# Ordering the first stage of a graph-network kernel: a second list planner, trace durations and a table of ranks

## The chip, the cores and the metric

The kernel runs on one core of a Trainium2 chip. A core has engines that run side by side, each through its own list of instructions in order: TensorE (PE) for matrix products, VectorE (DVE), ScalarE (ACT) and GpSimd (POOL) for elementwise work, and SyncE (SP), which here only issues DMA transfers. The metric is the device time of one execution in microseconds (us), as the median of several runs.

## The reference

The input is 128 batches of 128 tokens with 128 features (x) and a 0/1 adjacency matrix per batch. Four graph layers follow one another, each applied to a normalized, rectified copy of x and added to x. The first stage of the kernel, which the change is about, computes layer 0 and the first, costly part of layer 1:

```
# layer 0 (only relation 1 can occur in the given data)
h = relu(layernorm(x));  mask = (adj == r)
agg = sum over r of (mask / degree) @ h @ rel_weights[r]
x = x + relu(layernorm(agg + h @ self_w.T + self_b))
# layer 1, first part
h = relu(layernorm(x))
D = abs(h[:, :, None, :] - h[:, None, :, :])     # all pairs of tokens of a batch
p = D @ W1.T + b1                                # 128 features -> 64
m, v = mean and variance of p over all batches and pairs
```

The statistics m and v need all pairs of all batches. So the values of p are stored, and a second stage can start only when the last of them has been counted. The second stage computes the scores, the softmax and the output of layer 1, a third one layers 2 and 3.

## The kernel before

**Groups and tiles.** A group is G = 4 batches, and there are NG = 32 groups. A batch has NT = 4 tiles of pair differences, each [128 features, 2 x 8 x 128 pairs], so a group has 16 tiles, and tile i belongs to batch i // 4 with t = i % 4. As the pairs are symmetric, only about half of them are formed.

**Steps of a tile** (`pairs`, five per tile): "d", the difference of tokens (`difference`, L361; t = 1 and 3 on GpSimd, t = 0 and 2 on DVE, where one operand is read from the PSUM tile XP); "abs", the absolute value on ScalarE (`absolute`, L409), except for t = 0, which takes a maximum in place of the difference; "hp", the products on PE into a PSUM tile (`products`, L371, and for t = 0 also L374, which adds a linear part with weights "xw"); "hs", the copy of that PSUM tile to an SBUF buffer z by ScalarE (`evacuate`, L385); "st", the statistics of z on DVE (`statistics`, L399 to L406). There are two buffers of d for each of the two engines and two PSUM tiles "hp". Each half batch of z is stored to HBM ("out0", "out", L392) out of a ring of ten buffers.

**Steps of a group's chain** (`chain`, and `features` for each half of the group): layer 0 and the normalizing of its result. In order: load x and adj; the mask, moments and roots (GpSimd L493, DVE L483 and L485, GpSimd L272 to L331), the centred copy "hn" (ACT L506), transposes and products on PE with copies by ACT between them ("pt", "hT", "pm", "maskT", "ph", "hw", "po"; L516 to L530), "o", "mvo", "rso", "oc", "on", "end", then "mvx", "rsx" and two steps "h1" (ACT L547). For each half: "xp" (PE, two transposes into XP, L439), "xe" (ACT, copy, L443), "again" (GpSimd, L456), "pw" (PE, L447, into other columns of the same XP bank) and "xw" (ACT, L451, reads these columns). The chain of a later group is worked beside the tiles of an earlier one.

**What sets the order.** Each step is recorded with `step(name, engine, cost, after, rank, work)`. `_ordered` then makes a plan: it keeps a time for each engine, takes the engine that can start earliest, on it the step that can start first, and among those that could start at the same time the one of the lowest rank. A step can start when the steps it names in `after` are done, plus HOP1 = 0.4 us if they ran on another engine. `takes` and `gives` count the two PSUM banks "sm". The plan is the order in which the program issues the instructions, and so the order on each engine. Nothing at run time follows its times. Ranks count tiles: for example, d of tile i has rank i - 2 or i - 3, abs i - 1, hp i, hs i + 1, st i + 2. A step of the chain has s0 plus a number, with s0 = 16 g - 31.

A second planner, `_ranked`, stands in the same file and orders the third stage. It differs in this: an engine becomes free LATE[engine] before a step's end (DVE 0.08, ACT and PE 0.1, GpSimd 0.02 us); the hop is HOPS = 0.1 us; a tile's products count as done DEEP = 0.25 us after their end; a DMA counts as landed after a time by its kind; banks are given as a list of holds (which step takes one, which steps have to read it before it is free); and among the steps that could start within a margin of the first, the lowest rank is taken.

Of the kernel before, what the change touches and what calls it, by code (L numbers as in the profile page):

```python
# [18 lines left out]
G = 4  # L19
# [20 lines left out]
HOP1 = 0.4  # L40
HOPS, DEEP, ARRIVING, NEAR = 0.1, 0.25, 2.4, 0.025
LATE = {"SP": 0.0, "Pool": 0.02, "ACT": 0.1, "DVE": 0.08, "PE": 0.1}
LANDED = {"load": 6.0, "out": 5.0, "out0": 5.0}
# [51 lines left out]


def _ordered(steps, limits, hop):

    named = {s[0]: s for s in steps}
    free, done = dict.fromkeys(("SP", "Pool", "ACT", "DVE", "PE"), 0.0), {}
    left = {tag: [0.0] * n for tag, n in limits.items()}
    waits = {s[0]: [a for a in s[3] if a in named] for s in steps}
    followers, ready = {}, {e: {} for e in free}
    for name, after in waits.items():
        for a in after:
            followers.setdefault(a, []).append(name)
    missing = {name: len(after) for name, after in waits.items()}

    def released(name):
        engine = named[name][1]
        ready[engine][name] = max([0.0] + [done[a] + hop * (named[a][1] != engine) for a in waits[name]])

    for name, n in missing.items():
        if n == 0:
            released(name)
    plan = []
    while len(plan) < len(steps):
        best = None  # L120
        for engine, names in ready.items():
            could = []
            for name, since in names.items():
                takes = named[name][4]
                if all(left[tag] for tag in takes):
                    could.append((max([free[engine], since] + [min(left[tag]) for tag in takes]),
                                  named[name][6], name))
            if could:
                first = min(could)[0]
                one = min((c for c in could if c[0] == first), key=lambda c: c[1])  # L130
                if best is None or first < best[0]:
                    best = one
        start, _, name = best
        _, engine, cost, _, takes, gives, _, work = named[name]
        del ready[engine][name]
        free[engine] = start + cost
        done[name] = start + cost + (LANDING if engine == "SP" else 0)
        for tag in takes:
            left[tag].remove(min(left[tag]))
        for tag in gives:  # L140
            left[tag].append(start + cost + hop)
        plan.append(work)
        for f in followers.get(name, ()):
            missing[f] -= 1
            if missing[f] == 0:
                released(f)
    return plan
# [63 lines left out]
def tile_gnn_stack(ctx: ExitStack, tc: tile.TileContext, a: dict, out: bass.AP):  # L211
# [96 lines left out]
    def two_stages(general):  # L308
# [6 lines left out]
        with tc.tile_pool(name="c0", bufs=1) as c0, tc.tile_pool(name="p0", bufs=2) as p0:  # L315
# [29 lines left out]
            def step(name, engine, cost, after, rank, work, takes=(), gives=()):  # L345
                steps.append((name, engine, cost, after, takes, gives, rank, work))
# [64 lines left out]
            def pairs(i):  # L411

                b, t = divmod(i, NT)
                n, by_max = b // 2, t == BY_MAX
                engine, cost, rank = ("Pool", 4.22, i - 3) if t in ON_POOL else ("DVE", 2.2, i - 2)
                step(("d", i), engine, cost, [("again", n), ("d", i - 2), ("hp", i - 4 + 2 * general)], rank, lambda: difference(i))
                if not by_max:
                    step(("abs", i), "ACT", 1.8, [("d", i)], i - 1, lambda: absolute(i))
                step(("hp", i), "PE", 3.44 if by_max else 1.72,
                     [("d" if by_max else "abs", i), ("hp", i - 1), ("hs", i - 2)] + [("xw", n)] * by_max,  # L420
                     i, lambda: products(i))
                step(("hs", i), "ACT", 0.9, [("hp", i), ("hs", i - 1)]
                     + [("st", i - 4 * NT), ("out", b - ahead_by // 2)] * (t % 2 == 0), i + 1, lambda: evacuate(i))
                step(("st", i), "DVE", (1.3 if b % G < G - 1 else 2.4) if t == NT - 1 else 1.21, [("hs", i), ("st", i - 1)], i + 2,
                     lambda: statistics(i))
                if t == 1 and b < NB - G:
                    step(("out0", b), "SP", 0.4, [("hs", i)], i + 1.5, lambda: kept(b, 0))
                if t == NT - 1 and b < NB - G:
                    step(("out", b), "SP", 0.4, [("hs", i)], i + 1.5, lambda: kept(b, 1))

            def features(g, half):
# [21 lines left out]
                step(("xp", n), "PE", 0.35, [("h1", g, half), ("xw", n - 2)] + tiles(n - 2), s0 + 0.5, turned)  # L453
                step(("xe", n), "ACT", 0.3, [("xp", n), ("pw", n - 3)] + tiles(n - 3), s0 + 0.6, copied)
                step(("again", n), "Pool", 0.3, [("xe", n)], s0 + 1,
                     lambda: nc.gpsimd.tensor_copy(XE[n][:, :, P:], XE[n][:, :, 0:2 * KH]))  # L456
                step(("pw", n), "PE", 0.5, [("xe", n)], s0 + 1.5, weighed)
                step(("xw", n), "ACT", 0.18, [("pw", n)] + [("hp", NT * b) for b in (2 * n - 6, 2 * n - 5)], s0 + 2, negated)

            def chain(g):  # L460
# [89 lines left out]
                step(("load", g), "SP", 1.2, [("h1", g - 2, 1), ("x", g - 2), ("xp", 2 * g - 5)] * (general or g > 3),  # L550
# [3 lines left out]
                begun = own("load") + ([("rsx", 0)] if g == 1 else [("hp", 12 * g - 22)] if g in (2, 3) else [])  # L554
                step(("mask", g), "Pool", 1.5, begun, s0 + 1, masked)
                step(("mv", g), "DVE", 1.05, begun, s0 + 3, lambda: moments("x"))
                step(("deg", g), "DVE", 0.6, own("mask"), s0 + 3.1, degree)
                step(("rs", g), "Pool", 1.95, own("mv"), s0 + 5, roots)
                step(("most", g), "Pool", 0.25, own("deg"), s0 + 5.1, at_least)
                step(("per", g), "DVE", 0.15, own("most"), s0 + 7, lambda: nc.vector.reciprocal(t["deg"], t["deg"]))  # L560
                step(("hn", g), "ACT", 1.55, own("rs"), s0 + 7, lambda: centred("hn", "x", AF.Relu))
                step(("share", g), "Pool", 1.05, own("per"), s0 + 9, shared)
                step(("pt", g), "PE", 0.55, own("hn"), s0 + 9, lambda: turned("hn"), takes=("sm",))
                step(("hT", g), "ACT", 0.5, own("pt"), s0 + 9.5, lambda: copied("hT", "pt"), gives=("sm",))
                step(("pm", g), "PE", 0.55, own("share", "hT"), s0 + 11, lambda: turned("mask"), takes=("sm",))
                step(("maskT", g), "ACT", 0.5, own("pm"), s0 + 12, lambda: copied("maskT", "pt"), gives=("sm",))
                step(("ph", g), "PE", 1.05, own("hT") + ["small"], s0 + 11.1, projected, takes=("sm",))
                step(("hw", g), "ACT", 0.5, own("ph"), s0 + 13, lambda: copied("hw", "ph"), gives=("sm",))
                step(("m8", g), "Pool", 0.65, begun, s0 + 11,
                     lambda: nc.gpsimd.tensor_scalar(M8[g], t["adj"], 2, 0, op0=OP.min, op1=OP.max))  # L570
                step(("po", g), "PE", 2.05, own("maskT", "hw"), s0 + 14, gathered, takes=("sm",))
                step(("o", g), "DVE", 0.6, own("po", "agg") + ["selfb"], s0 + 15, joined, gives=("sm",))
                step(("mvo", g), "DVE", 1.05, own("o"), s0 + 15.1, lambda: moments("o"))
                step(("rso", g), "Pool", 1.95, own("mvo", "hn"), s0 + 17, roots)
                step(("oc", g), "ACT", 1.55, own("rso"), s0 + 18, lambda: centred("o", "o"))
                step(("on", g), "DVE", 1.25, own("oc") + ["on_all"], s0 + 20, scaled, takes=("sm",))
                step(("end", g), "DVE", 0.62, own("on"), s0 + 21, ended, gives=("sm",))
                step(("x", g), "SP", 0.4, own("end"), s0 + 21.1, lambda: nc.sync.dma_start(X[g], t["x"]))
                step(("mvx", g), "DVE", 1.05, own("end"), s0 + 21.1, lambda: moments("MV1"))
                step(("rsx", g), "Pool", 1.95, own("mvx", "oc", "m8"), s0 + 23, lambda: roots(True))  # L580
                for half in range(2):
                    step(("h1", g, half), "ACT", 0.78, own("rsx") + [("xp", 2 * g - 5)] + [("h1", g, 0)] * half,
                         s0 + 25 + half, lambda half=half: h1(half))
# [47 lines left out]
            step("on_all", "PE", 0.6, ["small", ("pt", 0)], -98, on_all, takes=("sm",))  # L631
            step("selfb", "ACT", 0.6, ["on_all"], -98, in_group, gives=("sm",))
# [45 lines left out]
            if general:  # L678
                with tc.manual_schedule():
                    for work in _ordered(steps, {"sm": 2}, HOP1):  # L680
                        work()
                steps.clear()
                relations()
# [69 lines left out]
            with tc.manual_schedule():  # L753
                for work in _ordered(steps, {"sm": 2}, HOP1):
# [912 lines left out]
```

## Time and profile before

| what | value |
|---|---|
| median of 3 runs (lowest to highest) | 2720.53 us (2718.41 to 2720.79) |
| the profiled execution | 2717.82 us |
| span of its trace | 2716.0 us |
| granted clock of TensorE, mean | 0.98 |
| busy over the span: PE, DVE, ACT, POOL | 90%, 91%, 87%, 62% |
| first d on DVE | 34.37 us |
| end of the first stage's last statistics on DVE | 1498.7 us |
| second stage's first activation (L883) | 1504.25 us |

The span runs from the first to the last instruction. In the profile, a group line names the source line, the engine, the operation, the tiles (written <- read), their shapes, the count, then the busy time in us and the mean duration in ns, and after the second bar the idle time of the engine just before these instructions with what ended it. A wait line names the engine and the tile that waited, what it waited for, the sum in us, how often, and the longest. In the timeline, a line has start and duration in us, the instruction, and in brackets the idle time before it. Matmul ends are modelled. Line numbers are those of the kernel before.

### The profile page before, as it was taken

To read this page: it belongs to the slowest core of one execution; us is meant where nothing else is said; L and a number is where in the kernel's file an instruction comes from. 1 tells how busy PE (TensorE), PEld (TensorE's weight loads), DVE (VectorE), ACT (ScalarE), POOL (GpSimd) and SP (SyncE) were. 2 spreads that over 40 slices of the span, in tenths; PEclk is the share of its full clock that TensorE was granted. 3 is DMA by queue.
4 is the path that set the end of the run, shared out by engine and by line. 5 is a ranking of instruction groups with operands and counts; after the bars stand their busy time and mean duration, and the time that the engine had idled before them with its cause. 6 is when DMAs were issued, how large, how long until landed. Compare 5 with 4: busy or idle time off the path is not lost.

```text
span 2716.0 us, 41908 instructions
## 1 busy us (share of the span) xinstructions
PE 2431.7 (90%) x14521; PEld 1169.3 (43%) x14521; DVE 2477.9 (91%) x4738; ACT 2375.6 (87%) x2821; POOL 1690.9 (62%) x1628
## 2 busy tenths in 40 slices
PE   6999999999999999999998788888888896999997
PEld 3333333333333333333333344444444444777776
DVE  5999999999999999999999799988888887899997
ACT  5999999999999999999999777788777774999996
POOL 6999999999999999999988001001001003656663
PEclk8999999999999999999999899999999998999998
DMA  3455555555555555555543799999999992021211
GB/s 115 180 200 199 203 201 202 208 199 209 198 209 198 209 198 204 203 198 203 200 201 132 297 409 408 387 410 410 411 410 409 411 402 94 21 67 55 63 36 33
DMA packets 185426, 611.43 MB, mean 225 GB/s; under 512 B 31987, under 2 KB 99702, under 8 KB 121718
## 3 DMA queue, kind: packets, MB, share of 16 engines
q1 hardware_dynamic: 184768, 608.50, 58.1%
q8 instruction: 118, 1.93, 0.3%
q14 instruction: 102, 0.84, 0.1%
q10 hardware_dynamic: 438, 0.17, 0.0%
HBM read 312.58 MB, written 296.03 MB: 224 GB/s over the span
## 4 chain that ended last, share of the span: by engine, by line
ACT 33%; PE 21%; DVE 19%; issue 11%; DMA 10%; POOL 6%; SPq 0%; ACTq 0%; POOLq 0%; DVEq 0%
ACT z L385 11%; ACT d L409 11%; PE hp L371 5%; PE ps L858 4%; DMA rows<-sk 4%; DVE z L901 3%; DMA z<-hp 3%; DVE d L361 3%; DMA u<-rows 3%; PE hp L374 2%; POOL d L361 2%; ACT o L506 2%; PE pk L865 2%; ACT h L547 2%; ACT hn L506 1%
## 5 line engine op out<-in xcount | busy, mean ns | idle before, releaser
L361 POOL TENSOR_TENSOR d<-xe 128x2048 f32<-128x2048 f32 x256 | 1073.9, 4200 | 68.7 <-PE hp L371 51.5
L371 PE MATMUL hp<-d,w1T 128*64 128x512 f32 x4096 | 997.1, 601 | 105.5 <-ACT z L385 87.8
L409 ACT ACTIVATE d<-d 128x2048 f32<-128x2048 f32 x384 | 735.5, 1935 | 9.6 <-POOL d L361 5.8
L361 DVE TENSOR_TENSOR d<-xe,xp 128x2048 f32<-128x2048 f32 x256 | 579.3, 2263 | 7.1 <-PE hp L371 4.1
L371 PEld LDWEIGHTS hp<-d,w1T 128*64 128x64 f32 x4096 | 286.6, 136 | 621.0 <-issue 462.8
L385 ACT COPY z<-hp 128x1024 f32<-128x1024 f32 x512 | 517.0, 1028 | 37.1 <-PE hp L374 33.8
L949 POOL TENSOR_TENSOR x<-x,bt 128x512 f32<-128x512 f32 x32 | 45.7, 1428 | 681.8 <-DMA x<-x 399.8
L399 DVE BATCH_NORM_STATS2 st<-z 128x6 f32<-128x512 f32 x512 | 349.5, 683 | 43.2 <-ACT z L385 43.0
L400 DVE BATCH_NORM_STATS2 st<-z 128x6 f32<-128x512 f32 (+1 forms) x512 | 329.4, 643 | 0.0
L901 DVE SCALAR_TENSOR_TENSOR z<-z 128x2048 f32<-128x2048 f32 x128 | 294.8, 2303 | 7.2 <-ACT z L883 6.7
L883 ACT ACTIVATE z<-z,bias,scale 128x2048 f32<-128x2048 f32 x128 | 267.2, 2087 | 9.6 <-DVE bias L795 7.9
L887 ACT ACTIVATE zr<-z,bias,scale 128x2048 f32<-128x2048 f32 x128 | 267.4, 2089 | 0.5 <-DMA z<-hp 0.5
L374 PE MATMUL hp<-both_t,xw 128*64 128x512 f32 x1024 | 267.7, 594 | 0.0
L858 PE MATMUL ps<-z,w2z 128*32 128x512 f32 x1024 | 141.9, 626 | 65.3 <-DVE z L901 64.5
L865 PEld LDWEIGHTS pk<-pick,su 128*128 128x128 f32 x1024 | 125.1, 192 | 143.9 <-DVE su L879 104.8
L865 PE MATMUL pk<-pick,su 128*128 128x16 f32 x1024 | 137.5, 266 | 30.4 <-DVE su L879 29.4
L374 PEld LDWEIGHTS hp<-both_t,xw 128*64 128x64 f32 x1024 | 81.2, 138 | 140.0 <-issue 140.0
L858 PE MATMUL ps<-zr,w2r 128*32 128x512 f32 x1024 | 139.5, 617 | 0.0
L858 PE MATMUL ps<-z,w2l 128*32 128x512 f32 x1024 | 139.1, 612 | 0.0
L1558 PE MATMUL pv<-wr,e 128*128 128x128 f32 x1024 | 134.0, 278 | 2.0 <-ACT wr L1483 1.1
L1558 PEld LDWEIGHTS pv<-wr,e 128*128 128x128 f32 x1024 | 124.1, 192 | 8.3 <-ACT wr L1483 1.5
L1442 ACT ACTIVATE h<-x,nb,rs 128x128 f32<-128x128 f32 x256 | 105.5, 489 | 20.6 <-POOL nb L1437 17.8
(241 smaller groups left out, 3785.9 us busy)
## 6 DMA issues: line engine op xcount, KB each, us to landing
hp<-z SPq DMA_DIRECT2D x248, 1024.0 KB, 3.9
z<-hp SPq DMA_DIRECT2D x248, 1024.0 KB, 13.5
x<-x SPq DMA_DIRECT2D x118, 256.0 KB, 7.7
u<-rows SPq DMA_DIRECT2D x32, 384.0 KB, 11.6
x<-in_x_dram SPq DMA_DIRECT2D x32, 256.0 KB, 5.6
adj<-in_adj_dram SPq DMA_DIRECT2D x32, 256.0 KB, 5.8
out_dram<-x SPq DMA_DIRECT2D x32, 256.0 KB, 2.4
z<-y SPq DMA_DIRECT2D x27, 256.0 KB, 11.9
```

The lines of the kernel that those rows point to most:

```text
L361: eng.tensor_tensor(d, ahead, x[:, None, None, :].to_broadcast([P, 2, KC, P]), OP.max if t == BY_MAX else OP.subtract)
L371: nc.tensor.matmul(hp[64 * hh:64 * hh + 64, c:c + 512], w1T2 if by_max else w1T, d[:, hh, c:c + 512], start=True, stop=not by_max, skip_gr ...
L374: nc.tensor.matmul(hp[64 * hh:64 * hh + 64, c:c + 512], XW[i // NT // 2][:, i // NT % 2, :], both_t.rearrange("p h k i -> p h (k i)")[:, h ...
L385: nc.scalar.copy(half_of(b, t), linear.pop(i))
L399: nc.vector.bn_stats(st[:, 2 * t, :], hs[:, 0:512])
L400: nc.vector.bn_stats(st[:, 2 * t + 1, :], hs[:, 512:1024 - P * last])
L409: nc.scalar.activation(diffs[i], diffs[i], AF.Abs)
L858: nc.tensor.matmul(ps[32 * c:32 * c + 32, :], w[:, w0:w0 + 32], v[:, 512 * c:512 * c + 512], start=j0 == 0, stop=w is w2r, skip_group_chec ...
L865: nc.tensor.matmul(pk[:, kk, 0:16], su[:, kk, :], pick.rearrange("p h j -> p (h j)"), start=True, stop=True)
L883: nc.scalar.activation(z0, z0, AF.Identity, bias=bias1, scale=scale1[:, 0:1])
L887: nc.scalar.activation(zr, z1, AF.Relu, bias=bias1, scale=scale1[:, 0:1])
L901: nc.vector.scalar_tensor_tensor(z0, z0, 0.01, z0, op0=OP.mult, op1=OP.max)
```

## The change

The first stage is planned with `_ranked` in place of `_ordered`, which is removed with HOP1:

```diff
-                    for work in _ordered(steps, {"sm": 2}, HOP1):
+                    for work in _ranked(steps, {"sm": 2}, taken, HOPS, NEAR):
```

(at both places where the stage is planned; the first of them is for data that this input doesn't have). NEAR = 0.025 us was in the file already, and so were the other constants of `_ranked`. The holds of "sm" are a list of pairs, and `takes` and `gives` leave the steps:

```diff
+TAKEN = (("pt", "hT"), ("pm", "maskT"), ("ph", "hw"), ("po", "o"), ("on", "end"))
...
+            taken = [("sm", (a, g), [(b, g)]) for g in range(NG) for a, b in TAKEN] + [("sm", "on_all", ["selfb"])]
```

The rank that a step names is replaced by one from a table: 16 for each group, plus a number that depends on the step, and for tiles on the position in the group (0 to 15), for `features` on the half. Steps that the table doesn't have (the constants' loads, the fetch) keep theirs:

```diff
+RANK1 = {"small": 5.5, "on_all": -21, "selfb": -88.5, "both_t": 69.5, "fold": 22.5, "zero": 86.5, "xp": (25, 6.5),
+         "xe": (-73.5, 2), "again": (30.5, -38), "pw": (38, -59), "xw": (84, 10.5), "load": 14, "mask": 8.5,
+         "mv": 80.5, "deg": -48, "rs": -7, "most": -70, "per": 38.5, "hn": 21.5, "share": -74.5, "pt": 14,
+         "hT": -24, "pm": -81.5, "maskT": 22.5, "ph": 19, "hw": 36, "m8": -10.5, "po": -82, "o": 88, "mvo": 36,
+         "rso": -75.5, "oc": -23.5, "on": 62, "end": -58.5, "x": -53, "mvx": 54.5, "rsx": -54.5,
+         "h1": (-13, -93.5),
+         "d": (48.5, 10, -31.5, -34.5, -16.5, -63, -6, 36, 58.5, -27, -180, -50, -73.5, -31, 64, -37.5),
+         "hp": (72.5, -76.5, 26, -8, 34.5, -30, -54, 43.5, 18.5, -53, 1, 6.5, -22, -157, -120, 31),
+         "hs": (-114.5, -49, 10.5, -47, 55, -49, -39, -106, -123, 81, -8, -22, -42, -6.5, 17, -105),
+         "st": (-5, 6.5, -4, -3.5, -137.5, -143, 69, -12.5, 117, -194.5, -100, 126, -35, -10.5, -62.5, 20.5),
+         "abs": (-29.5, 55.5, -114, 8, 2, 59.5, -12.5, 6, -22, 21.5, 3.5, -62.5),
+         "out0": (-10.5, -14, -143.5, 23.5), "out": (-10.5, 126, -63.5, 12.5)}
...
-            def step(name, engine, cost, after, rank, work, takes=(), gives=()):
-                steps.append((name, engine, cost, after, takes, gives, rank, work))
+            def step(name, engine, cost, after, rank, work):
+                of, n = (name, 0) if isinstance(name, str) else name[:2]
+                if of in RANK1:
+                    per = 16 if of in ("d", "abs", "hp", "hs", "st") else 4 if of in ("out", "out0") else \
+                        2 if of in ("xp", "xe", "again", "pw", "xw") else 1
+                    at = n % per - (of == "abs") * (n % per // NT + 1) if per > 1 else name[2] if of == "h1" else 0
+                    rank = 16 * (n // per) + (RANK1[of][at] if isinstance(RANK1[of], tuple) else RANK1[of])
+                steps.append((name, engine, cost, after, rank, 0.0, work))
```

The costs become durations as the trace has them, for instance:

```diff
-                engine, cost, rank = ("Pool", 4.22, i - 3) if t in ON_POOL else ("DVE", 2.2, i - 2)
+                engine, cost, rank = ("Pool", 4.2, i - 3) if t in ON_POOL else ("DVE", 2.26, i - 2)
...
-                    step(("abs", i), "ACT", 1.8, [("d", i)], i - 1, lambda: absolute(i))
-                step(("hp", i), "PE", 3.44 if by_max else 1.72,
+                    step(("abs", i), "ACT", 1.92, [("d", i)], i - 1, lambda: absolute(i))
+                step(("hp", i), "PE", 3.54 if by_max else 1.82,
...
-                step(("hs", i), "ACT", 0.9, [("hp", i), ("hs", i - 1)]
+                step(("hs", i), "ACT", 1.0, [("hp", i), ("hs", i - 1)]
...
-                step(("pw", n), "PE", 0.5, [("xe", n)], s0 + 1.5, weighed)
-                step(("xw", n), "ACT", 0.18, [("pw", n)] + [("hp", NT * b) for b in (2 * n - 6, 2 * n - 5)], s0 + 2, negated)
+                step(("pw", n), "PE", 0.66, [("xe", n)], s0 + 1.5, weighed)
+                step(("xw", n), "ACT", 0.29, [("pw", n)] + [("hp", NT * b) for b in (2 * n - 6, 2 * n - 5)], s0 + 2, negated)
```

and likewise for the chain. One dependency of the plan changes, the one that says when a group's chain may begin:

```diff
-                begun = own("load") + ([("rsx", 0)] if g == 1 else [("hp", 12 * g - 22)] if g in (2, 3) else [])
+                begun = own("load") + ([("rsx", 0)] if g == 1 else [("h1", g - 2, 1)])
```

No instruction, buffer or tile shape changes, and the two later stages keep their code and their plans.

## Prediction

> **What bounds the kernel now.** I read the page first: no engine stands out over the whole span, and the engines are shared by stages.
>
> ```profile
> PE 2431.7 (90%) x14521; PEld 1169.3 (43%) x14521; DVE 2477.9 (91%) x4738; ACT 2375.6 (87%) x2821; POOL 1690.9 (62%) x1628
> ...
> L361 POOL TENSOR_TENSOR d<-xe 128x2048 f32<-128x2048 f32 x256 | 1073.9, 4200 | 68.7 <-PE hp L371 51.5
> L371 PE MATMUL hp<-d,w1T 128*64 128x512 f32 x4096 | 997.1, 601 | 105.5 <-ACT z L385 87.8
> L409 ACT ACTIVATE d<-d 128x2048 f32<-128x2048 f32 x384 | 735.5, 1935 | 9.6 <-POOL d L361 5.8
> L361 DVE TENSOR_TENSOR d<-xe,xp 128x2048 f32<-128x2048 f32 x256 | 579.3, 2263 | 7.1 <-PE hp L371 4.1
> ```
>
> Three lines of code, L361, L371 and L409, spread the first stage over four engines. So the second view is busy time by stretch. In the chain of waits "PE hp L371 x12" recurs at 200.33, 245.94, 291.57 ... 1386.46 us: one group of four batches every 45.62 us. I cut at such marks.
>
> ```profile
> core 0: us, PE busy (x) PEld busy (x) DVE busy (x) ACT busy (x) POOL busy (x), PEclk, DMA share, GB/s
> 382.81:747.77 364.96, 339.98 (x1632) 132.00 (x1633) 353.86 (x609) 347.21 (x377) 339.05 (x209) 1.00 0.54 203
> 747.77:1158.35 410.58, 382.47 (x1836) 148.46 (x1837) 398.10 (x685) 390.62 (x424) 381.17 (x235) 1.00 0.53 202
> 1158.35:1386.46 228.11, 212.48 (x1020) 82.48 (x1021) 221.17 (x381) 217.02 (x236) 211.81 (x131) 1.00 0.53 202
> ```
>
> These 1003.65 us are 22 groups. Per group DVE is busy 973.13/22 = 44.23 us, ACT 43.40, PE 42.50, POOL 42.37, of 45.62. DVE is the first bound, 97% full. DMA at 0.53 is none. The third view, waits over 25 groups (245.94 to 1386.46), says what the missing 1.39 us of DVE are:
>
> ```profile
> PE hp L371 <- ACT z L385: 64.6, 128, 0.9
> POOL d L361 <- PE hp L371: 33.1, 82, 0.8
> DVE st L399 <- ACT z L385: 32.1, 50, 1.0
> ACT z L385 <- PE hp L374: 29.9, 25, 1.3
> ACT xw L451 <- DVE d L361: 22.2, 25, 0.9
> ```
>
> DVE waits twice a group, 32.1/25 = 1.28 us, always for ScalarE's copy of a tile out of PSUM (step "hs"); 0.11 us are small gaps. The fourth view, the timeline of one group, shows the longer of the two (DVE, then ACT, then PE):
>
> ```profile
> 763.00 0.67 DVE L400 BATCH_NORM_STATS2 st<-z 128x6 f32<-128x512 f32 x1
> 764.64 0.69 DVE L399 BATCH_NORM_STATS2 st<-z 128x6 f32<-128x512 f32 x1 [0.97 <-ACT z L385]
> ...
> 761.04 0.59 ACT L519 ACTIVATE maskT<-pt 128x512 f32<-128x512 f32 x1
> 761.52 0.38 ACT L443 COPY xe<-xp 128x256 f32<-128x256 f32 x1
> 761.77 1.93 ACT L409 ACTIVATE d<-d 128x2048 f32<-128x2048 f32 x1
> 763.59 1.02 ACT L385 COPY z<-hp 128x1024 f32<-128x1024 f32 x1
> ...
> 758.76 1.94 PE L371 MATMUL hp<-d,w1T 128*64 128x512 f32 x8 [0.18 <-ACT z L385]
> ```
>
> PE had finished that tile at 760.70; ScalarE did maskT, xe and an absolute value first and copied it at 763.59. That is the order and nothing else: with the copy ahead of the 1.93 us absolute value, DVE would not have waited. The other wait (0.31 us, at 782.55) is different: there the copy starts as soon as PE is done, so an earlier product is needed.
>
> **What the Trainium skill says.** (1) "Perfetto Trace Analysis", Identifying the Most-Contended Engine: occupancy is a fair measure of closeness to the limit for Vector, Scalar and GpSimd, not for matmuls. Here that makes DVE's 97% a hard floor, and leaves PE's 93% uncertain. (2) Same page, DVE / Act Engine Instruction: the reported end is the write's acknowledgement, later than the point from which the next instruction may start. The trace agrees: 747.53 + 0.68 = 748.21, but the next DVE instruction starts at 748.13. The new plan has this as an occupancy 0.08 us shorter than the duration. (3) "SBUF — State Buffer", Who interferes with whom: a DVE instruction with at most one SBUF input doesn't contend with GpSimd. DVE's d reads one operand from PSUM, and the trace agrees: all of them took 2222 to 2289 ns, and GpSimd's 4180 to 4234, whatever ran beside. So another order leaves the 44.23 us as they are. (4) "PSUM — Partial Sum Buffer", PSUM bank collisions: two engines mustn't touch one bank at once, even at other columns, so a dependency is put between them. The trace agrees: "xw" (ScalarE, a bank of XP) waited for a d on DVE (same bank) 31 times of 64, 29.5 us. Neither plan lists this dependency.
>
> **The change, part by part.** No instruction is added or removed; in stage one only the order on each engine changes.
> - Costs. Net of the early release, old and new agree: d on DVE 2.26 - 0.08 = 2.18 against 2.2, absolute value 1.92 - 0.10 = 1.82 against 1.8, copy 1.0 - 0.1 = 0.9 against 0.9. Alone worth nothing: the loads were right already.
> - Hand-over. 0.4 us becomes 0.1 plus the early release, and 0.25 more after the tile products. The trace: copy end 764.62 to DVE start 764.64; copy end 747.63 to PE start 747.77. With 0.4 the old plan was pessimistic, and its sequence fits the chip only roughly. Worth alone: between 0 and the whole 1.28 us per group.
> - Ranks. A table by position replaces the tile index and so decides between a copy and an absolute value that could both start. With the hand-over this is the item that can move the waits above.
> - "sm" as holds: the same two banks, released by the same readers. 0.
> - `begun`: groups 2 and 3 may start their chain after h1 of group g-2 (31.3 us for group 2) and not after a tile product; from group 4 on the load waits for that anyway. It can put a 1.51 us mask ahead of the first GpSimd d at 34.42, or fill DVE's start (3.13 + 1.57 + 1.03 us idle at 34 to 48): -3 to +3 us, once. I take 0.
> - SP queue: its stores, loads and constants are resequenced too. Each store lands 3.9 us after issue, DMA is at 0.53 and the queue idles most of the time: 0. If a store sat behind a load that waits, ScalarE's copies would stop for want of a z buffer; ten halves of 5.7 us each (45.62/8) cover it.
> - Drain: from 1448 to 1499 no chain is left, and DVE waits about 6.5 us (0.75, 0.64, 0.43, 0.23, 0.32, 0.80, 1.26, 1.43, 0.66). -3 to +3; I take 0.
> - Later stages: their code is the same. Stage two's first activation at 1504.25 follows the statistics, so everything moves up with stage one's end. 0.
>
> Sum. Groups run at the period from 60 to about 1448 us: 1388/45.62 = 30.4. The floor is 44.23 + 0.11 = 44.34, a gain of 1.28 x 30.4 = 38.9 us. I don't expect all: at 44.34 ScalarE would be 98% full and may idle 0.94 us, where it now waits 1.19 (products) + 0.89 (xw) = 2.08. About half of those 2.08, 1.04, would have to remain on the chip's count because of (4) and because two PSUM tiles tie PE to ScalarE: 43.40 + 0.14 (its small gaps, 45.62 - 43.40 - 2.08) + 1.04 = 44.58. DVE's own residue is bounded by 0 and 1.28; I take 0.5, a little above the 0.24 that ScalarE alone imposes. Period 44.34 + 0.5 = 44.84; saved 0.78 x 30.4 = 23.7 us. The profiled execution took 2717.82 us (2716.0 of span and 1.8 around it) and would be 2694.1. The median of the runs is 2720.53, 2.7 above it, and gives 2696.8, say 2697.
>
> **Rivals.**
> - *Whole gain*: 38.9 us, with up to 6 from start and drain: 2676 to 2682, say 2680. For it: the waits are few and of order alone. Against: four engines at 96 to 99% on two d buffers and two PSUM tiles.
> - *Wait moved* (or the order hardly changes): the copy goes ahead, the absolute value comes later, PE starves and the next copy is late. PE's 2.6 us per group of waiting for copies (64.6/25) speak for it. Between 0.33 us per group saved and 0.18 lost: 2710 to 2726, say 2717.
> - *Slower: the PSUM bank that the plan doesn't know.* The table ranks xw of a first half at 84 and pw at 38, late among ready steps, so they may be emitted behind a d on the same bank and wait up to its 2.27 us, with ScalarE's copies queued behind xw and PE's products behind pw. Today one xw in two waits, 0.89 us. If both do: ScalarE 43.40 + 0.14 + 1.19 + 1.78 = 46.51, +0.89 x 30.4 = +27 us: 2748. It decides once ScalarE's waits in sum pass 2.08 us a group. Against: a later xw also often meets a finished d.
>
> **Numbers.** 2697 is the likeliest case, 0.60, own range 2684 to 2709. Whole gain 0.17, moved 0.12, slower 0.11. The range 2677 to 2719 leaves out the slower case, the upper third of "moved" and a little below the floor. 0.2% is 5.4 us, about what a measurement of this kernel can tell from no change; below 2715.1 lie the first two cases and 0.05 of "moved": faster 0.82, same 0.07, slower 0.11.
>
> **What would show it.** Right: a mark every 44.5 to 45.1 us, DVE's busy time still 44.2 per group, "DVE st <- ACT z" below 0.8 us per group, ScalarE's two waits together near 1.0, stages after 1500 us of unchanged length. Wrong: DVE's busy time per group changed (then durations depend on order); xw or pw waiting longer than 0.9 us per group (bank); gain sitting in start or drain; a second stage that isn't merely shifted.

## The result, and the profile after

| | before | after |
|---|---|---|
| median | 2719.64 us (4 runs, 2718.41 to 2720.79) | 2676.21 us (4 runs, 2676.06 to 2676.36) |
| profiled execution, span | 2717.82, 2716.0 us | 2676.09, 2674.2 us |
| one group in the middle of stage one | 45.62 us | 44.15 us |
| stage one's last statistics end | 1498.7 us | 1454.0 us |

The ratio is 0.984, 95% interval 0.9823 to 0.9857: 43.4 us faster. The forecast was 2697 in a range of 2677 to 2719; the time lies 0.8 us below that range, at the forecast's "whole gain" case.

The page of the changed kernel, with the rows that answer to those of before (L328 is the old L361, L338 the old L371, L376 the old L409, L352 the old L385, L366 the old L399):

```profile
PE 2437.0 (91%) x14521; PEld 1162.1 (43%) x14521; DVE 2469.6 (92%) x4738; ACT 2380.3 (89%) x2821; POOL 1706.1 (64%) x1628
...
L328 POOL TENSOR_TENSOR d<-xe 128x2048 f32<-128x2048 f32 x256 | 1073.8, 4205 | 36.4 <-PE hp L338 34.5
L338 PE MATMUL hp<-d,w1T 128*64 128x512 f32 x4096 | 994.1, 601 | 57.6 <-ACT z L352 54.5
...
L366 DVE BATCH_NORM_STATS2 st<-z 128x6 f32<-128x512 f32 x512 | 354.7, 693 | 6.2 <-ACT z L352 6.1
```

The same instructions, with about half the idle time ahead of GpSimd's d and PE's products; ahead of DVE's statistics it is 6.2 us where it was 43.2. Busy time of 22 groups (the columns are those shown of before):

```profile
362.27:715.50 353.23, 340.40 (x1634) 129.04 (x1632) 352.40 (x609) 348.31 (x378) 338.14 (x209) 1.00 0.56 210
715.50:1112.90 397.40, 382.99 (x1838) 145.15 (x1836) 396.46 (x686) 391.86 (x425) 380.48 (x235) 1.00 0.55 209
1112.90:1333.61 220.71, 212.73 (x1022) 80.64 (x1020) 220.19 (x381) 217.65 (x237) 211.31 (x131) 1.00 0.54 209
```

Per group DVE is busy 969.05/22 = 44.05 of 44.15 us, 99.8%; ACT 43.54, PE 42.55, POOL 42.27. The waits over these 22 groups, all that are listed for the four engines:

```profile
ACT d L376 <- POOL d L328: 10.1, 22, 0.5
PE hp L338 <- ACT z L352: 32.7, 66, 0.9
POOL d L328 <- PE hp L338: 17.6, 44, 0.6
```

A line gives the engine and tile that waited, for what, the sum in us, how often, and the longest. DVE has no wait there; one gap of 0.10 us per group is left. "xw" doesn't wait for a d any more (1.1 us in all over 64, for other things). The timeline shows how. Here are DVE and ScalarE at tile 11, the place in a group where the longer wait of before stood.

```profile
744.40 2.30 DVE L328 TENSOR_TENSOR d<-xe,xp 128x2048 f32<-128x2048 f32 x1
746.59 0.72 DVE L366 BATCH_NORM_STATS2 st<-z 128x6 f32<-128x512 f32 x1
...
740.42 1.01 ACT L352 COPY z<-hp 128x1024 f32<-128x1024 f32 x1
```

The copy ends at 741.43 and its statistics start at 746.59, 5.2 us later; before, they started 0.03 us after their copy. It is so for all tiles of these groups: the statistics start 5.5 us after their copy in the mean and never less than 3.6, where before it was 1.7 and at the least 0.03. A tile takes 44.15/16 = 2.8 us, so DVE now has about two copied tiles in stock, and a copy that is late by one absolute value (1.9 us) no longer stops it.

**Where the 41.8 us of the spans come from.** DVE's work is the same, so I split its time into busy and idle. To the end of stage one: busy 1422.2 -> 1416.0, idle 76.5 -> 38.0, together -44.7 us. Of it, -41.76 lies in the 28 periods from the end of the first group's statistics to the end of the 29th's (idle -35.56, busy -6.20). Up to the end of the first group's it is +4.53, and in the last three groups -7.47. Everything after stage one adds +2.90.

The start shows one rank of the table at work. Here are GpSimd and, in the last line, DVE at the first tiles:

```profile
34.54 0.29 POOL L423 COPY xe<-xe 128x128 f32<-128x128 f32 x1
34.79 0.61 POOL L537 TENSOR_SCALAR m<-adj 128x512 uint8<-128x512 int32 x1
...
38.41 0.29 POOL L423 COPY xe<-xe 128x128 f32<-128x128 f32 x1
...
38.73 4.48 DVE L328 TENSOR_TENSOR d<-xe,xp 128x2048 f32<-128x2048 f32 x2 [4.04 <-POOL xe L423]
```

"again" has rank +30.5 for a first half and -38 for a second, so of the first group's two copies the second half's goes first, at 34.54, and chain work of groups 1 and 2 goes ahead of the other. The first d starts at 38.73 and not at 34.37. It costs little. Up to the first group's statistics DVE's idle time is even 0.6 us less than before (29.0 against 29.6), because it does 5.1 us of later groups' chains there; the last three groups have that much less to do.

### The profile page after: what moved, and what is told of

Read it like the earlier page. It is cut to its first block, busy times and chain, and to the rows that moved or that the text cites. A ratio compares the mean times of both kernels' runs of the same rounds, so it can differ in the third digit from the quotient of the medians.

```text
span 2674.2 us, 41925 instructions
## 1 busy us (share of the span) xinstructions
PE 2437.0 (91%) x14521; PEld 1162.1 (43%) x14521; DVE 2469.6 (92%) x4738; ACT 2380.3 (89%) x2821; POOL 1706.1 (64%) x1628
## 4 chain that ended last, share of the span: by engine, by line
PE 37%; ACT 24%; DVE 15%; DMA 12%; POOL 7%; issue 4%; SPq 0%; POOLq 0%; DVEq 0%; ACTq 0%
PE hp L338 16%; ACT d L376 9%; ACT z L352 7%; DMA z<-hp 4%; PE hp L341 4%; DMA rows<-sk 4%; PE ps L825 4%; POOL d L328 4%; DMA u<-rows 3%; DVE z L868 3%; ACT o L473 2%; PE pk L832 2%; ACT hn L473 2%; PE xp L414 1%; DVE e L1502 1%
## 5 line engine op out<-in xcount | busy, mean ns | idle before, releaser
L328 POOL TENSOR_TENSOR d<-xe 128x2048 f32<-128x2048 f32 x256 | 1073.8, 4205 | 36.4 <-PE hp L338 34.5
L338 PE MATMUL hp<-d,w1T 128*64 128x512 f32 x4096 | 994.1, 601 | 57.6 <-ACT z L352 54.5
L376 ACT ACTIVATE d<-d 128x2048 f32<-128x2048 f32 x384 | 733.8, 1924 | 19.8 <-POOL d L328 19.5
L328 DVE TENSOR_TENSOR d<-xe,xp 128x2048 f32<-128x2048 f32 x256 | 583.6, 2280 | 7.0 <-POOL xe L423 4.0
L352 ACT COPY z<-hp 128x1024 f32<-128x1024 f32 x512 | 519.1, 1015 | 9.7 <-PE hp L338 4.5
L338 PEld LDWEIGHTS hp<-d,w1T 128*64 128x64 f32 x4096 | 276.9, 136 | 559.5 <-issue 455.3
L366 DVE BATCH_NORM_STATS2 st<-z 128x6 f32<-128x512 f32 x512 | 354.7, 693 | 6.2 <-ACT z L352 6.1
L367 DVE BATCH_NORM_STATS2 st<-z 128x6 f32<-128x512 f32 (+1 forms) x512 | 336.4, 657 | 0.0
```

The source lines that it names most:

```text
L328: eng.tensor_tensor(d, ahead, x[:, None, None, :].to_broadcast([P, 2, KC, P]), OP.max if t == BY_MAX else OP.subtract)
L338: nc.tensor.matmul(hp[64 * hh:64 * hh + 64, c:c + 512], w1T2 if by_max else w1T, d[:, hh, c:c + 512], start=True, stop=not by_max, skip_gr ...
L352: nc.scalar.copy(half_of(b, t), linear.pop(i))
L366: nc.vector.bn_stats(st[:, 2 * t, :], hs[:, 0:512])
L367: nc.vector.bn_stats(st[:, 2 * t + 1, :], hs[:, 512:1024 - P * last])
L376: nc.scalar.activation(diffs[i], diffs[i], AF.Abs)
```

## The experiments

All were compared with the kernel before, run on the same chip; numbers per group are from each run's profile, the 22 groups in the middle.

**1. The new planner without the table.**

```diff
-                if of in RANK1:
+                if of in ():
```

> The changed kernel with the old ranks (tile index) in place of the table; the trace durations, the 0.1 us hand-over, the holds and the new planner stay. Theory 1, the sequence that the table encodes is the gain: the planner's own arithmetic with these ranks gives 45.38 us per group against 45.51 for the old plan, so the time should be near 2715 us (2708 to 2720), with two DVE waits per group left. Rival, the pessimistic hand-over of 0.4 us was what cost (the prediction's part on the hand-over, worth up to 1.28 us per group): 2680 to 2695.

Measured: 2707.03 us against 2717.27, ratio 0.996 (0.9943 to 0.9978); 45.27 us per group, with 45 waits of DVE for a copy in 22 groups, 12.9 us in sum. This is just below the range of theory 1 and far from the rival. Added in this order, planner, costs, hand-over, landing times and `begun` together are worth about 10 us and the table the other 33. The costs alone weren't run.

**2. The table with one old dependency.** `begun` as before for groups 2 and 3.

> The changed kernel with the table, but with the old dependency for when the chains of groups 2 and 3 may begin. Prediction's part: this edit matters once, at the start, by -3 to +3 us: 2673 to 2679. Theory 1, stronger form (the table is one fitted sequence and not a set of preferences; a small shift at the start makes the planner fall into another cycle): its arithmetic gives 46.17 us per group against 44.30, so 30 groups x 1.87 = +56 us: about 2732, slower than the kernel before.

Measured: 2740.82, ratio 1.0081 (1.0065 to 1.0098), slower than the kernel before. The groups don't settle: from one group's last statistics to the next one's they go round 48.2, 47.0, 46.9, 50.1, 40.4 and 43.5 us again and again, 46.0 in the mean of a round. The "-3 to +3 us, once" of my part list was wrong by a factor of twenty: the edit concerns two groups, but it sends the planner into another sequence for all that follow.

**3. The table alone in the old planner.** The table and the lines that look it up, in the kernel before.

> The kernel before with the table of ranks alone: old planner, old costs, 0.4 us hand-over, old start. If the ranks are good preferences by themselves (rival): 2680 to 2700. If they fit only the planner and costs with which they were found (theory 1): its arithmetic gives 47.95 us per group against 45.51, +2.44 x 30 = +73 us: about 2793.

Measured: 2770.95, ratio 1.0192 (1.0175 to 1.0209), 47.57 us per group. This is somewhat less bad than expected, but the ranks aren't good preferences by themselves. DVE's waits in 22 groups, the two longest:

```profile
DVE st L417 <- ACT z L403: 28.6, 23, 2.1
DVE lnst L501 <- DMA x<-in_x_dram: 27.8, 21, 2.3
```

The first, 1.30 us per group, is about what it was before. The second, 1.26, is new: the moments of x wait for the load of x. It is a part of the change that my list had left out: the old planner counts a load as landed 3.0 us after its issue, the new one 6.0, and the profile shows 5.6 in both kernels. The table with the landing time alone wasn't run.

**4. The hand-over alone.**

```diff
-HOP1 = 0.4
+HOP1 = 0.1
```

> The kernel before with one number changed: the plan's hand-over between engines is 0.1 us in place of 0.4; old planner, old costs, old ranks. If the pessimistic hand-over is a good part of the loss: the planner's arithmetic gives 44.83 us per group against 45.51, -0.68 x 30 = -20 us, about 2697. If that arithmetic is too hopeful, since without an allowance for what a hand-over really takes the planned starts come too early, the chip gives less: 2705 to 2718.

Measured: 2764.73 against 2720.91, ratio 1.0164 (1.0147 to 1.0181): outside both expectations, slower. It takes 46.95 us per group where the planner's arithmetic said 44.83. ScalarE's waits in 22 groups:

```profile
ACT xw L451 <- DVE d L361: 34.5, 21, 2.8
ACT z L385 <- PE hp L374: 20.6, 22, 1.2
```

The wait of my slower rival is here: xw waits for a d in the same PSUM bank, 1.57 us per group where it was 0.89 before, and no plan lists that dependency. ScalarE's waits sum to 3.2 us per group (with 8.5 and 6.0 us for other things), beyond the 2.08 from which the rival was to decide. But xw's wait grew by 0.7 us per group and the period by 1.3, and DVE waits 0.3 us per group for loads of x here too. What of the slowdown is due to xw and what to the other waits wasn't tested.

**5. One exchange in the old plan.** In each group the copy of tile 11 ahead of the absolute value of tile 13:

```diff
+    for i in range(16 + 11, 496, 16):
+        at = [n for n, _ in plan]
...
+        copy, late = at.index(("hs", i)), at.index(("abs", i + 2))
+        if late < copy:
+            plan.insert(late, plan.pop(copy))
```

> The kernel before with one exchange per group in its finished plan: the copy of tile 11 of a group goes ahead of the absolute value of tile 13 that stood before it on ScalarE. My reading of the timeline (the longer DVE wait is order alone): the 0.97 us wait goes, DVE is the bound, 30 x 0.97 = -29 us: about 2691. Rival, the wait moves (the absolute value comes 0.9 us later, PE's product of tile 13 and the next copies with it): 2712 to 2724.

Measured: 2712.96 against 2717.27, ratio 0.9978 (0.9972 to 0.9985); 45.44 us per group. DVE's waits in 22 groups:

```profile
DVE d L372 <- POOL xe L467: 17.1, 22, 0.8
DVE st L410 <- ACT z L396: 7.1, 22, 0.4
```

The wait that I had called "the order and nothing else" went, as the prediction said. But 0.78 us a few steps later took its place: DVE's next d reaches its turn earlier and waits for "again", which stands behind two d on GpSimd (753.74 to 762.1 us). So 0.18 of 0.97 us is gained: behind the wait that one exchange removes, another limit lies only 0.18 us away. Other single exchanges weren't tried.

**6. The PSUM bank in the new order.** Each first half's xw (groups 1 to 29) is issued behind the d on its bank:

```diff
+            weights, tile = at.index(("xw", n)), at.index(("d", 2 * NT * n))
+            if weights < tile:
+                plan.insert(tile, plan.pop(weights))
```

> The changed kernel with one step per group moved in its finished plan: the negated weights xw of a group's first half are issued after the d on VectorE that reads the same PSUM bank, so that ScalarE waits for that d as the prediction's slower rival said. Theory (the rival's mechanism is real, its price is what passes ScalarE's slack of about 0.5 us per group): a wait of 0.5 to 2.2 us per group, so 0 to +1.7 us per group against the changed kernel: 2676 to 2726, about 2690. Rival (no bank dependency of any weight, ScalarE has slack): 2674 to 2679.

Measured: 2678.03, ratio 0.9843 (0.9826 to 0.9859), within noise of the changed kernel; 44.23 us per group. xw waited for a d 4 times, 4.6 us, in the first groups only. Later each d is over when ScalarE gets there. In the trace stage one ends at 1460.1 us and not at 1454.0: the 4.6 us once, and about 0.08 us per group. So the dependency is real, and in this order it costs at most that little; it is far from the +27 us of the slower rival.

**7. More work on one engine.** One more copy of 128x448 per group, on DVE ahead of "end" or on ScalarE after "hw":

```diff
+                    nc.vector.tensor_copy(spare, t["on"].rearrange("p a b -> p (a b)")[:, 0:448])
```

> The changed kernel with one more VectorE copy per group (128x448 out of PSUM into a spare tile that nothing reads), placed ahead of the step end; the plan is unchanged. Theory (VectorE is the only bound, with no slack left): it costs its whole occupancy, about 0.53 us per group, 31 x 0.53 = +16 us: about 2692. If slack were left: less than +5 us.

> The changed kernel with one more ScalarE copy per group (128x448 out of PSUM into a spare tile that nothing reads), after the step hw; the plan is unchanged. Theory (VectorE is the bound and ScalarE has 0.5 us of slack per group): the 0.45 us are nearly hidden: 2676 to 2681. Rival (with four engines above 95% any delay comes through): +0.45 x 31 = +14 us: about 2690.

Measured: DVE 2687.34 (0.9875, 0.9858 to 0.9891), 44.67 us per group, +0.51 for an instruction of 0.61 us (0.53 without the overlap): nearly all of it comes through. ScalarE 2684.07 (0.987, 0.9854 to 0.9887), 44.50 per group, +0.35 for one of 0.55 us (0.45 without the overlap): much closer to the rival, nothing like hidden. Most of ScalarE's idle time isn't slack.

**8. Less work on DVE.** The row sum of the mask, 0.59 us of DVE's time per group, is left out; the degree is a constant instead, which GpSimd sets (in the changed kernel and in the one before) or DVE itself:

```diff
-                    nc.vector.tensor_reduce(t["deg"], t["mask"], AX.X, OP.add)
+                    nc.gpsimd.memset(t["deg"], 8.0)
```

> The changed kernel, its plan unchanged, with VectorE's row sum of the mask left out (the degree is set to a constant by GpSimd, so the result is not the reference's): 0.59 us of VectorE occupancy less per group. Theory (VectorE alone bounds the changed order): -0.59 x 29 = -17 us: about 2659. Rival (the order is as tight on PE, ScalarE and GpSimd as on VectorE, as the run with more ScalarE work suggests): -1 to -6 us, 2670 to 2675.

> The kernel before with the same 0.59 us of VectorE work per group left out (the degree is a constant). Theory (its order, a loop of waits over several engines, sets 45.62 us, and VectorE has 1.28 us of slack in it): -4 to 0 us, 2714 to 2719. Rival (VectorE bounds it as it bounds the changed kernel): -17 us, about 2702.

> The changed kernel with the row sum replaced by a constant that VectorE itself sets, so that GpSimd has nothing added (in the earlier run it had 0.11 us per group); the result is not the reference's. Theory (a second loop over GpSimd, ScalarE and PE is about 44.05 us long, and the 0.11 us on GpSimd lengthened it to 44.16): 44.03 to 44.08 us per group. Rival (some loop of exactly 44.15 us that doesn't run through GpSimd's chain work): 44.15 again. If neither: below 43.8, VectorE alone bounds and the earlier run was held by the constant on GpSimd only.

Measured: 2674.96 for the changed kernel (0.9841, 0.9825 to 0.9856, against 0.984 for it complete), 44.16 us per group; 2719.63 for the one before (1.0001, 0.9993 to 1.0009), 45.64 per group. With the constant on DVE, a single execution, it is 44.13 per group. So before, DVE's work was no limit at all, as expected. After, against my theory, it isn't the only one: taking 0.6 us from it gives nothing or 0.02. What holds the kernel instead can be read from the chain of waits of one group of the last kernel. It runs from PE to ScalarE and back, and no piece of DVE or GpSimd is in it (9.6% is "issue", for which the profile names no cause):

```profile
725.07 1.94 PE hp L338 x8
...
737.85 1.89 PE hp L338 x8
...
740.67 1.91 ACT d L376
742.59 1.53 ACT hn L473 x4
744.12 0.82 ACT z L352
...
749.27 0.90 ACT z L352
750.22 1.08 PE hp L338 x4
```

PE's products wait for ScalarE to empty one of the two PSUM tiles (32 us in 22 groups, as in the changed kernel), and ScalarE's copies come between its other work. The chain of one group of the changed kernel runs through the same pieces, without DVE too. If this loop takes the 44.13 us and DVE's work 44.15, two bounds lie within 0.02 us of each other. That is a reading of the chain, not a test of it: the only run that lengthened this loop is the one with more ScalarE work, where 0.35 of 0.45 us came through, and none shortened it. The theory on GpSimd's 0.11 us fell too: 44.13 lies above its 44.03 to 44.08.

**9. A better start and end.** 61 ranks of single steps in the first and last groups replaced:

> The changed kernel with 61 ranks of single steps in the first and last groups replaced, found with the planner's own arithmetic: 2.5 us less to the end of stage one. If that arithmetic holds to 2 us: 2672 to 2675; if not, within 3 us of the changed kernel either way.

Measured: 2671.02, ratio 0.9823 (0.981 to 0.9836), the lowest of all; but its interval overlaps that of the changed kernel. In the trace stage one ends 1.1 us earlier and not 2.5; two groups near the end, the 26th and 27th, take 48.1 and 45.0 us. The rest of the difference lies in the later stages, whose code is the same. It isn't shown to be better.

## Why the prediction was right and wrong

**Right: the mechanism.** DVE's waits for copies were a matter of order, nothing else was needed, and their removal is the gain: its idle time falls by 35.6 us in 28 periods. The pace of an instruction didn't depend on the order. The durations that the profile reports grew a little (d 2263 to 2280 ns on DVE, 4200 to 4205 on GpSimd, the first statistics 683 to 693), but on DVE the overlap with the next instruction grew as well: over the 22 groups the instruction behind a d starts 2.18 us after it in both traces, the one behind a full statistics 0.60 before and 0.59 after. Start and drain were smaller terms.

**Wrong: the residue of 0.5 us per group.** The step "I don't expect all ... DVE's own residue is bounded by 0 and 1.28; I take 0.5" failed. Of the 0.5, 0.24 rested on ScalarE keeping half of its 2.08 us of waits; the rest was a margin with no sum behind it. ScalarE kept 10.1/22 = 0.46, for a d on GpSimd, and none of the waits that I had counted. Products are waited for no more, and xw's wait is gone because a half is prepared earlier. These are the first d of a half and its xw before, and the xw of the same half after:

```profile
765.90 2.27 DVE L361 TENSOR_TENSOR d<-xe,xp 128x2048 f32<-128x2048 f32 x1
768.21 0.28 ACT L451 ACTIVATE xw<-xp 128x128 f32<-128x128 f32 x1 [0.89 <-DVE d L361]
...
736.77 0.33 ACT L418 ACTIVATE xw<-xp 128x128 f32<-128x128 f32 x1
```

Before, xw comes 2.3 us behind the start of that d; after, 7.6 us ahead of it (it starts at 744.40, as shown above). The residue on DVE is 0.00. That is 0.5 x 30.4 = 15 us, the greatest part of the miss of 20.6.

**Wrong: the hard floor of 44.34.** "So another order leaves the 44.23 us as they are" held for the pace of each instruction and not for the busy time. To call it a hard floor was my step, more than the "fair measure" on which it leaned. The busy time counts overlapping instructions once. Back to back, an instruction of DVE starts 0.08 us before the end of the one ahead of it (0.10 in the changed kernel); after a wait there is no such overlap. At the wait of before, 1.05 us pass between the start that would have been (763.59) and the real one, of which the profile calls 0.97 idle and 0.08 busy. Without waits busy fell to 44.05: 0.18 x 30.4 = 5.5 us more. The range ended at 2677, a few us below what that floor allows (2720.5 - 38.9 = 2681.6); 5.5 us more were too many, and so the time fell out of it by 0.8 us.

The two terms make 21 us, nearly the whole miss. That the rest cancels is luck: the forecast added 2.7 us because the median before lay so far above the profiled execution, where the changed kernel's lies 0.1 above; and the second stage took 2.9 us more.

**Wrong as a list of parts: hand-over, ranks, `begun`, each with its own price.** Experiments 1 to 4 give about -10 us for the new planner without the table, +54 for the table without the planner, +44 for the hand-over alone, and +65 against the changed kernel for one old dependency of two groups. They are no sum: together the parts make one sequence. Here is the planner's own arithmetic against the chip, in us per group:

| kernel | plan | chip |
|---|---|---|
| before (0.4 us hand-over) | 45.51 | 45.62 |
| hand-over 0.1 alone | 44.83 | 46.95 |
| table in the old planner | 47.95 | 47.57 |
| new planner, old ranks | 45.38 | 45.27 |
| the same with the table, old `begun` | 46.17 | 46.02 |
| changed kernel | 44.30 | 44.15 |

With the new arithmetic the plan is within 0.15 us of the chip, with 0.4 us it is within 0.4, and with 0.1 us alone it is off by 2.1. So "with 0.4 the old plan was pessimistic" doesn't show in the period of the kernel before, where the plan lies 0.11 us below the chip. The shorter hand-over alone made the kernel slower; with the planner, the costs and the landing times that came with it, it was 10 us faster (experiments 4 and 1). Whether such ranks could be found with the old arithmetic wasn't tried.

**Open: the second stage.** "Everything moves up" left out +2.9 us. From its first activation to the start of its last statistics it takes 781.6 us before and 784.3 after; in the other twelve profiles, with the same code there, 780.7 to 787.4. The 2.9 us are within that spread.

**The rivals.** "Whole gain" is what happened, at 0.17 and 2680. "Wait moved" is what one exchange does (experiment 5). The wait of the slower one grew in experiment 4, with its share in the slowdown untested, and it costs little in this sequence (experiment 6).

## What to carry to other kernels

When an engine stands at 97% and waits a little each round, find out whether one exchange frees it before you price the rest: here one gave 0.18 of 0.97 us, a whole new sequence all of it, with about two tiles between producer and consumer. Take as floor the start-to-start time of back-to-back instructions, not busy time with waits in it. This table of ranks goes with its planner and its dependencies: each of the two runs that changed one of them was slower than the kernel before. Search again after such a change.

## What was not expected of the hardware

An engine busy 99.8% of the time need not be the only limit: 0.53 us more on DVE cost 0.51, 0.59 less gave at most 0.02. By the chain of waits, a loop of PE and ScalarE is about as long. And on DVE less work lowered busy time by less: with the constant on GpSimd, 0.59 us left out took only 44.05 - 43.72 = 0.33 off. DVE has three gaps in a group there in place of one; at 0.08 us of lost overlap each, the two new ones explain 0.16 of the 0.26 that are missing, and the rest is open.
